# A four-layer graph network on one core: in each APPNP step, the sums of the last 9 node blocks by gathered rows beside products for the other 40

## The chip, the cores and the metric

The kernel runs on one core of a Trainium2 chip. A core has five engines with queues of their own: TensorE (PE, matmuls and transposes), VectorE (DVE), ScalarE (ACT), GpSimd (POOL; in this kernel it issues the gathers, that is DMAs whose addresses come from a list of row numbers) and SyncE (SP, which issues the other DMAs). The metric is device time in microseconds (us), lower is better, as the median of several runs. One more execution is taken by the profiler, and every row of a view below is from that one.

## The reference

A graph of 6250 nodes and 100000 edges (sorted by target `dst`), 128 features a node, passes through four layers, each of the form `x = x + layer(relu(layernorm(x)))`. The first is a mean over neighbours with a batch norm, the second a relational convolution (L1), the third an attention layer (L2). The change is in the fourth (L3), ten steps of APPNP:

```python
def _appnp(x, src, dst, norm, n_nodes):
    h = x
    def step(xk, _):
        msg = norm[:, None] * xk[src]
        agg = jax.ops.segment_sum(msg, dst, num_segments=n_nodes)
        return ((1.0 - ALPHA) * agg + ALPHA * h, None)
    xK, _ = jax.lax.scan(step, x, None, length=K)      # K = 10, ALPHA = 0.1
    return xK
...
src = jnp.concatenate([src, loop])                     # loop = arange(n): a self loop for each node
dst = jnp.concatenate([dst, loop])
...
norm = deg_inv_sqrt[src] * deg_inv_sqrt[dst]
return jax.nn.relu(_appnp(x, src, dst, norm, n))
```

So each step sums, for each node, the rows of its neighbours and its own, and mixes the first state in. The result of a step is what the next one reads.

## The kernel before

Nodes are padded to 49 blocks of 128 (`W`, 49). The kernel keeps z, the state times the root of the inverse degree, so that a step is z' = 0.9 / degree x (sum of z over edges and the self loop) + 0.1 x z of the start. The sum is a matrix product with the count matrix of edges. This matrix is made once, during the first layer, block of targets by block of targets (`stag`, L1006), and stored in DRAM as fp8 with the self loops added (`adj`, `looped`, L1018 to L1021). In the same stage the `chores` (L856) prepare lists of indices in pieces, between the blocks' products.

An L3 step (L1357 to L1403) runs over 13 groups of target blocks (`groups`, L1351: ten of 4, three of 3). For a group it goes over the 49 source blocks in 7 chunks of 7 (`GS`). A chunk is loaded from `adj` on SP (`am`, L1363; 448 KB for a group of four), turned from fp8 to fp32r into `ar` on ACT (L1370) or DVE (L1368) in turn, and multiplied: for each source block two matmuls, with the high and the low part of z (`xs`, L1374), so 98 matmuls for a group, all into one PSUM tile. `ar` has a pad of 128 behind each source block (`GD + 1`), and what is written of it are 7 pieces. Then ACT copies the sums (`y`, L1379), PE transposes them back (`yt`, L1382), DVE scales them and adds `hd` (0.1 x the first z, kept in SBUF as `by_node`; L1387), and `split2` (L1345) makes the new high and low parts with DVE, ACT and DVE. The parts are in two sets, `parts[0]` and `parts[1]`, read and written in turn. The last step applies relu, adds the kept x and stores the output (L1392 to L1402). The order on the engines is set by the framework's scheduler from the program's order and pools. POOL has no work in this stage.

Gathers are used in L1 and L2. `gather` (L686) reads 128 rows from a table in DRAM, one to a partition, for one column of a list of row numbers. In L1 (L1088 to L1099) the edges are cut into 128 equal runs, a lane for each partition. Step by step each lane gathers its next edge's row, scales it, and adds the sum so far if the edge has the target of the one before (`same`, L1097, `rows <- prev * same + rows`). The tiles of running sums are stored to a table (`scan1`); a node's sum is then the entry of its last edge, plus, where its edges begin in an earlier lane, what that lane ended with.

`general` (L83) computes all of it another way, for graphs whose tables overflow; flags (`over`, `redo`) decide between the two.

Of the kernel before, what the change touches and what calls it, by code (L numbers as in the profile page):

```python
# [10 lines left out]
F32 = mybir.dt.float32  # L11
I32 = mybir.dt.int32
BF16 = mybir.dt.bfloat16
F16 = mybir.dt.float16
AF = mybir.ActivationFunctionType
OP = mybir.AluOpType
AX = mybir.AxisListType
PSUM = bass.MemoryType.PSUM
DVE = mybir.EngineType.DVE

N = 6250
D = 128
E = 100000
P = 125
W = N // P
# [9 lines left out]
H = 8  # L35
# [6 lines left out]
K_STEPS = 10  # L42
ALPHA = 0.1
# [6 lines left out]
FW = 49  # L50
FN = FP * FW
# [11 lines left out]
LL = 782  # L63
LP = 128
# [8 lines left out]
F32R = mybir.dt.float32r  # L73
F8 = mybir.dt.float8e4
MULTI = 15
GD = 4
GS = 7
ENGINES = (mybir.EngineType.PE, mybir.EngineType.DVE, mybir.EngineType.Activation, mybir.EngineType.Pool,
# [553 lines left out]
def _fast(ctx, tc, a, out, pre):  # L632
    nc = tc.nc
    TT, TS, STT = nc.vector.tensor_tensor, nc.vector.tensor_scalar, nc.vector.scalar_tensor_tensor
    ident, eps, deg = pre["ident"], pre["eps"], pre["deg"]
    P, W = FP, FW
# [16 lines left out]
    def nodes(table):  # L653
        return table.rearrange("(w p) d -> p w d", p=P)
# [52 lines left out]

    table1 = dram.tile([FN * R, D], F32, name="ftable1")
# [4 lines left out]
    x_kept = dram.tile([FN, D], F32, name="x_kept")  # L713

    adj = dram.tile([W, P, W * P], F8, name="adj")
# [140 lines left out]
    def chores(sp):  # L856
# [6 lines left out]
        zero = sp.tile([LP, (LL + 2) * H // 4], F32, name="zero")  # L863
        nc.gpsimd.memset(zero, 0.0)
        for i in range(4):
            nc.sync.dma_start(begins.rearrange("(p q k) h -> q p (k h)", p=LP, q=4)[i], zero)
        nc.scalar.dma_start(scan1[ZROW:ZROW + 1, :], zero[0:1, :D])
        none = sp.tile([1, RW], F32, name="none")
# [42 lines left out]
        TS(end_row, row, float(ZROW), None, op0=OP.add)  # L911
        yield
# [8 lines left out]
    with tc.tile_pool(name="bxs", bufs=1) as bx, tc.tile_pool(name="bps", bufs=2, space=PSUM) as bps, \  # L921
# [64 lines left out]
        for w in range(W + 1):  # L986
# [29 lines left out]
            if w < W:  # L1016

                looped = bst.tile([P, P], F8, name="looped")  # L1018
                TT(looped, stag[:, w, :], eye, OP.add, saturate=False)
                nc.sync.dma_start(adj[w], stag.rearrange("p s d -> p (s d)"))  # L1020
                nc.sync.dma_start(adj[w][:, w * P:(w + 1) * P], looped)  # L1021
                behind = stag
# [221 lines left out]
    with tc.tile_pool(name="fl2f", bufs=2) as fp, tc.tile_pool(name="fl2fps", bufs=1, space=PSUM) as pp, \  # L1244
# [79 lines left out]
        def part5(b):  # L1324
            w0, n = blocks[b]
            t = fp.tile([P, 4, D], F32, name="z_hi")[:, :n, :]
            TS(t.bitcast(I32), z0[b].bitcast(I32), -4096, None, op0=OP.bitwise_and)
            nc.scalar.copy(parts[0][:, w0:w0 + n, 0, :], t)
            TT(parts[0][:, w0:w0 + n, 1, :], z0[b], t, OP.subtract)
            TS(by_node[:, w0:w0 + n, :], z0[b], ALPHA, None, op0=OP.mult)  # L1330
# [3 lines left out]
    mid.close()  # L1334


    hd = by_node
# [5 lines left out]
    parts.append(last.enter_context(tc.tile_pool(name="fl3x1", bufs=1)).tile([P, W, 2, D], F32R, name="xr1"))  # L1343

    def split2(pool, at, src):  # L1345
        t = pool.tile([P, D], F32, name="split_t")
        TS(t.bitcast(I32), src.bitcast(I32), -4096, None, op0=OP.bitwise_and)
        nc.scalar.copy(at[:, 0, :], t)
        TT(at[:, 1, :], src, t, OP.subtract)

    groups = [(w, 4) for w in range(0, 40, 4)] + [(w, 3) for w in range(40, W, 3)]  # L1351
    with tc.tile_pool(name="fl3a", bufs=3) as ap, tc.tile_pool(name="fl3c", bufs=3) as cp, \
            tc.tile_pool(name="fl3y", bufs=2) as yp, tc.tile_pool(name="fl3s", bufs=3) as sp, \
            tc.tile_pool(name="fl3ps", bufs=3, space=PSUM) as pp, \
            tc.tile_pool(name="fl3pt", bufs=2, space=PSUM) as pt, tc.tile_pool(name="fl3e", bufs=2) as ep:
        turn = 0
        for step in range(K_STEPS):  # L1357
            xs, new = parts[step % 2], parts[1 - step % 2]
            for w0, nd in groups:
                ps = pp.tile([D, GD * P], F32, name="dense3")  # L1360
                for s0 in range(0, W, GS):
                    am = ap.tile([P, GD, GS * P], F8, name="am")
                    nc.sync.dma_start(am[:, :nd, :],  # L1363
                                      adj[w0:w0 + nd, :, s0 * P:(s0 + GS) * P].rearrange("w p c -> p w c"))
                    ar = cp.tile([P, GS, GD + 1, P], F32R, name="ar")[:, :, :GD, :]
                    frm = am[:, :nd, :].rearrange("p w (s c) -> p s w c", c=P)
                    if turn % 2:
                        nc.vector.tensor_copy(ar[:, :, :nd, :], frm)  # L1368
                    else:
                        nc.scalar.copy(ar[:, :, :nd, :], frm)  # L1370
                    turn += 1
                    for i in range(GS):
                        for part in range(2):
                            nc.tensor.matmul(ps[:, :nd * P], xs[:, s0 + i, part, :],  # L1374
                                             ar[:, i, :nd, :].rearrange("p w c -> p (w c)"),
                                             start=(s0 + i == 0 and part == 0),
                                             stop=(s0 + i == W - 1 and part == 1))
                y = yp.tile([D, GD * P], F32, name="y3")
                nc.scalar.copy(y[:, :nd * P], ps[:, :nd * P])  # L1379
                yt = pt.tile([P, GD, D], F32, name="yt3")  # L1380
                for i in range(nd):
                    nc.tensor.transpose(yt[:, i, :], y[:, i * P:(i + 1) * P], ident)  # L1382
                if step < K_STEPS - 1:
                    for i in range(nd):
                        w = w0 + i
                        z = sp.tile([P, D], F32, name="z3")
                        STT(z, yt[:, i, :], d9[:, w:w + 1], hd[:, w, :], op0=OP.mult, op1=OP.add)  # L1387
                        split2(sp, new[:, w], z)
                    continue
                z = ep.tile([P, GD, D], F32, name="z3e")[:, :nd, :]  # L1390
                xb = ep.tile([P, GD, D], F32, name="x_back")[:, :nd, :]
                nc.sync.dma_start(xb, nodes(x_kept)[:, w0:w0 + nd, :])  # L1392
                for i in range(nd):
                    w = w0 + i
                    STT(z[:, i, :], yt[:, i, :], d9[:, w:w + 1], hd[:, w, :], op0=OP.mult, op1=OP.add)
                    nc.scalar.activation(z[:, i, :], z[:, i, :], AF.Relu, scale=back[:, w:w + 1])
                TT(xb, xb, z, OP.add)
                n = min(nd, full - w0)
                nc.sync.dma_start(nodes(out[0:full * P, :])[:, w0:w0 + n, :], xb[:, :n, :])
                if n < nd:  # L1400
                    nc.sync.dma_start(out[full * P:N, :], xb[:tail, n, :])
    last.close()  # L1402
    right.close()  # L1403
# [3 lines left out]
def gnn4_kernel(ctx: ExitStack, tc: tile.TileContext, a: dict, out: bass.AP):  # L1407
# [21 lines left out]
    with tc.tile_pool(name="csr", bufs=1) as sp, tc.tile_pool(name="csr2", bufs=4) as sp2, \  # L1429
# [87 lines left out]
        STT(over, most, float(HALO) + 0.5, over, op0=OP.is_gt, op1=OP.max)  # L1517
        bad_t = pp2.tile([1, EP], F32, name="p_ps")
# [67 lines left out]
```

## Time and profile before

| what | us |
| --- | --- |
| three runs | 6796.05, 6800.26, 6802.65 |
| their median | 6800.26 |
| the profiled execution | 6811.35 |
| its span, first to last instruction | 6809.6 |
| stage of L0 that builds `adj` (250 to 840) | 590 |
| the table of L1 (840 to 1220) | 380 |
| gathers of L1 (1220 to 2350) | 1130 |
| gathers of L2 (2510 to 3815) | 1305 |
| rest of L2 and the start of L3 (3815 to 4004.57) | 189.57 |
| the ten steps of L3, first to last matmul (4004.57 to 6799.20) | 2794.63 |

The stages were cut by hand from the timeline, and the busy time of each engine was then asked for each stage. Rows of groups of instructions have the line, the engine, the operation, out <- in with the program's names, shapes and count; behind the bar the busy time in all (us), the mean of one (ns), and the idle time of that engine just before such instructions with what ended it. A row of the timeline or of the chain of waits begins with its start and its length in us. PEclk is the share of the full clock that PE was granted: 1.00 in L3, 0.50 in the gather stages, 0.792 over the span.

### The profile page before, as it was taken

The numbers are of one execution on the slowest core, as the hardware profiler recorded it, in microseconds if no ns is written. First come the engines' busy times: TensorE is split into PE (matmuls) and PEld (weight loads), VectorE is DVE, ScalarE is ACT, GpSimd is POOL, SyncE is SP. The second block draws the span as 40 slices with busy tenths as digits, with TensorE's granted clock in tenths as the row PEclk, the third lists the DMA queues.
The fourth block names the chain that finished last, engine by engine and source line by source line (L and its number), as shares of the span: only waits on it lengthen the run. The fifth ranks groups of instructions, "written<-read, shape, count | busy, mean of one in ns | idle before, by whom it ended". The sixth has DMA issues, their size and how long they took to land.

```text
span 6809.6 us, 58963 instructions
## 1 busy us (share of the span) xinstructions
PE 3979.7 (58%) x19527; PEld 3092.1 (45%) x19527; DVE 3147.4 (46%) x7607; ACT 2727.3 (40%) x4424; POOL 1930.8 (28%) x1823
## 2 busy tenths in 40 slices
PE   3899899100000020000000379999999999999999
PEld 3466644000000010000000158888888888888888
DVE  7976543222222234545454654444444444444443
ACT  0667643222222220000000465555555555555555
POOL 1000000677777766776767400000000000000000
PEclk8799999555555555555555699999999999999999
DMA  2111166322222222322222234555545555455555
GB/s 62 65 69 68 64 268 289 133 99 93 93 96 90 89 63 79 100 89 91 95 93 89 76 95 138 145 140 143 141 138 144 143 141 143 138 145 141 141 154 146
DMA packets 590194, 805.02 MB, mean 118 GB/s; under 512 B 59275, under 2 KB 532626, under 8 KB 570422
## 3 DMA queue, kind: packets, MB, share of 16 engines
q1 hardware_dynamic: 521968, 677.37, 31.2%
q0 software_dynamic: 57728, 119.10, 6.4%
q10 hardware_dynamic: 10182, 4.69, 0.3%
q8 instruction: 155, 2.54, 0.2%
q14 instruction: 161, 1.32, 0.1%
HBM read 529.94 MB, written 274.22 MB: 118 GB/s over the span
## 4 chain that ended last, share of the span: by engine, by line
PE 54%; POOL 16%; DVE 11%; issue 9%; another core or an unknown queue 3%; ACT 2%; DMA 1%; POOLq 1%; DVEq 0%; SPq 0%; ACTq 0%
PE dense L1374 40%; POOL rows L687 15%; PE hr_ps L1074 5%; PE dense L955 5%; DVE rows L1231 3%; DVE rows L1215 2%; PE cnt_ps L1002 1%; PE yt L1382 1%; POOLq L687 1%; DVE rows L1209 1%; DVE far L1207 1%; ACT stag L1006 1%; DMA rows<-ftable,lane_src 0%; DVE fwr L916 0%
## 5 line engine op out<-in xcount | busy, mean ns | idle before, releaser
L1374 PE MATMUL dense<-ar,xr 128*128 128x512 f32 (+1 forms) x12740 | 2768.5, 378 | 20.7 <-ACT ar L1370 20.7
L1374 PEld LDWEIGHTS dense<-ar,xr 128*128 128x128 f32 x12740 | 2342.2, 188 | 398.4 <-ACT ar L1370 20.9
L1370 ACT CAST ar<-am 128x3584 fp32r<-128x3584 fp8e4 (+1 forms) x455 | 1373.1, 3018 | 834.1 <-PE dense L1374 633.8
L1368 DVE CAST ar<-am 128x3584 fp32r<-128x3584 fp8e4 (+1 forms) x455 | 987.2, 2170 | 1367.2 <-ACT ar L1370 1000.7
L687 POOL DMA_INDIRECT rows<-ftable,rel_l x822 | 876.6, 1066 | 1285.3 <-DMA w<-in_L_gnn_W_dram 1035.1
L687 POOL DMA_INDIRECT rows<-ftable,lane_src x822 | 883.8, 1075 | 403.4 <-issue 256.6
L1289 PE MATMUL ht_ps<-ident_p,h1g 128*128 128x128 f32 x49 | 9.8, 295 | 1333.5 <-ACT h1g L677 1333.2
L695 PE MATMUL ht_ps<-ident_p,long 128*128 128x128 f32 x49 | 16.5, 446 | 1193.1 <-issue 1183.6
L1094 ACT ACTIVATE rows<-rows,lane_norm 128x128 f32<-128x128 f32 x822 | 327.2, 401 | 811.3 <-DMA rows<-ftable,rel_l 651.6
L1097 DVE SCALAR_TENSOR_TENSOR rows<-rows,same 128x128 f32<-128x128 f32 x770 | 270.9, 352 | 805.6 <-issue 450.7
L1289 PEld LDWEIGHTS ht_ps<-ident_p,h1g 128*128 128x128 f32 x49 | 6.6, 144 | 1342.4 <-issue 1337.2
L695 PEld LDWEIGHTS ht_ps<-ident_p,long 128*128 128x128 f32 x49 | 9.9, 206 | 1199.4 <-issue 1187.0
L955 PE MATMUL dense<-xs,stag 128*128 128x384 bf16 x2401 | 448.5, 327 | 34.3 <-ACT stag L1006 34.1
L1006 ACT ACTIVATE stag<-cnt_ps 128x392 fp8e4<-128x392 f32 x784 | 381.7, 494 | 171.7 <-PE cnt_ps L1002 170.9
L1231 DVE SCALAR_TENSOR_TENSOR rows<-rows,same 128x136 f32<-128x136 f32 x770 | 271.9, 353 | 184.5 <-remote 60.1
L1074 PE MATMUL hr_ps<-fwr,ht 128*128 128x512 f32 x784 | 342.3, 597 | 6.2 <-ACT ht L697 6.2
L955 PEld LDWEIGHTS <-stag 128*128 128x128 fp8e4 x2401 | 227.3, 97 | 165.1 <-ACT stag L1006 45.2
L982 DVE TENSOR_TENSOR hot_v<-key_v,iota_v 128x1568 bf16<-128x1568 bf16 x196 | 190.8, 974 | 120.3 <-PE cnt_ps L1002 120.3
L1186 ACT COPY cut<-cut 128x136 f32<-128x136 f32 (+1 forms) x52 | 15.7, 305 | 570.3 <-DVE up L1199 273.0
L1074 PEld LDWEIGHTS hr_ps<-fwr,ht 128*128 128x128 f32 x784 | 148.8, 191 | 192.5 <-issue 180.3
L1077 DVE COPY hr<-hr_ps 128x512 f32<-128x512 f32 x196 | 135.6, 692 | 204.1 <-PE hr_ps L1074 201.6
L1215 DVE TENSOR_TENSOR rows<-rows 128x128 f32<-128x128 f32 x822 | 189.0, 284 | 47.4 <-issue 45.0
(268 smaller groups left out, 3292.3 us busy)
## 6 DMA issues: line engine op xcount, KB each, us to landing
am<-adj SPq DMA_DIRECT2D x700, 448.0 KB
ftable<-hr SPq DMA_DIRECT2D x49, 2048.0 KB
am<-adj SPq DMA_DIRECT2D x210, 336.0 KB
scan<-rows SPq DMA_DIRECT2D x51, 1152.0 KB
scan<-rows SPq DMA_DIRECT2D x51, 1024.0 KB
adj<-stag SPq DMA_DIRECT2D x49, 784.0 KB
rows<-ftable,rel_l POOLq DMA_INDIRECT x822
rows<-ftable,lane_src POOLq DMA_INDIRECT x822
```

What stands on the lines that cost most here:

```text
L687: nc.gpsimd.indirect_dma_start(out=tile_, out_offset=None, in_=table, in_offset=bass.IndirectOffsetOnAxis(ap=idx[:, k:k + 1], axis=0))
L955: nc.tensor.matmul(ps, stag[:, s, :], xs[:, s].rearrange("p t d -> p (t d)"), start=(s == 0), stop=(s == W - 1))
L982: TT(hot, k[:, :, None, :].to_broadcast(shape), iota[:, None, :, :].to_broadcast(shape), OP.is_equal)
L1006: nc.scalar.activation(stag[:, :, at:at + 2 * GN].rearrange("p s (g d) -> p g s d", g=2), ps[:, i, :2 * HG].rearrange("p (g s d) -> p g s ...
L1074: nc.tensor.matmul(ps, ht1[b][:, i * P:(i + 1) * P], wr[:, 4 * q:4 * q + 4, :], start=True, stop=True)
L1094: nc.scalar.activation(rows[:, t, :], rows[:, t, :], AF.Copy, scale=norm_l[:, k:k + 1])
L1097: STT(rows[:, t, :], prev, same[:, k:k + 1], rows[:, t, :], op0=OP.mult, op1=OP.add)
L1215: TT(rows[:, t, :D].rearrange("p (h c) -> p h c", h=H), rows[:, t, :D].rearrange("p (h c) -> p h c", h=H), rows[:, t, D:SW, None].to_broad ...
L1231: STT(rows[:, t, :SW], rows[:, t - 1, :SW], same[:, k0 + t:k0 + t + 1], rows[:, t, :SW], op0=OP.mult, op1=OP.add)
L1368: nc.vector.tensor_copy(ar[:, :, :nd, :], frm)
L1370: nc.scalar.copy(ar[:, :, :nd, :], frm)
L1374: nc.tensor.matmul(ps[:, :nd * P], xs[:, s0 + i, part, :], ar[:, i, :nd, :].rearrange("p w c -> p (w c)"), start=(s0 + i == 0 and part == ...
```

## The change

Products are made for the first 40 blocks of targets only (`DW`), in 10 groups of four: 70 chunks a step rather than 91. `adj` has 40 blocks. The sums of the last 9 blocks (`TW`) are made as in L1: the edges from number 81,440 (`E0`) on are cut into 128 lanes of 145 (`LE`), and a step gathers their rows from z in DRAM (`collect`, 29 tiles of 5 columns), runs the sum along each lane on DVE (`run_on`, 144 operations), stores the tiles to `scan3` and the lanes' ends to `carry3` (`put_down`), gathers the sums of the nodes' last edges and the carried sums (`fetch_ends`, 18 gathers), and adds the node's own row for the self loop (`add_up`). So z must also lie in DRAM, and every step stores it (`z_at`, two tables in turn); 0.1 x the first z is there too (`z_first`) and is fetched for each group, rather than kept in SBUF.

Other parts: `am` is loaded two chunks at a time (14 source blocks, 896 KB; the chunk 4 of a group alone), 40 loads a step. `ar` has no pad, so a chunk is written as one run of 3584 elements. Every third cast is on DVE, the others are on ACT. The first two groups do their chunks 0 to 4 before either does 5 and 6, which read the gathered blocks' parts of the step before. Splits work on a whole group (128x512) rather than a block. And the order on every engine is written out: each piece of work is put into `plan` with an expected time in chunks of products, the list is sorted by it, and the instructions are issued in this order with the scheduler off. In the `chores` come the lists of the new lanes, and a guard sends graphs with more than `128 x 145` edges in the last 9 blocks to `general`.

```diff
+GL = 14
+DW = 40
+TW = FW - DW
+LE = 145
+E0 = E - LP * LE
+LC = 5
...
+    z_at = [dram.tile([FN, D], F32, name=f"z_at{i}") for i in range(2)]
+    z_first = dram.tile([FN, D], F32, name="z_first")
+    scan3 = dram.tile([LP * LE + 1, D], F32, name="scan3")
+    carry3 = dram.tile([LP + 1, D], F32, name="carry3")
+
+    adj = dram.tile([DW, P, W * P], F8, name="adj")
...
+        dst_e = sp.tile([LP, LE], I32, name="dst_e")
+        nc.sync.dma_start(dst_e, a["dst"][E0:].rearrange("(p k) -> p k", k=LE))
+        nc.sync.dma_start(src_e, a["src"][E0:].rearrange("(p k) -> p k", k=LE))
...
+        nc.vector.memset(same_e[:, 0:1], 0.0)
+        TT(same_e[:, 1:], dst_e[:, 1:], dst_e[:, :LE - 1], OP.is_equal)
...
-            TS(by_node[:, w0:w0 + n, :], z0[b], ALPHA, None, op0=OP.mult)
+            nc.sync.dma_start(nodes(z_at[0])[:, w0:w0 + n, :], z0[b])
+            t = fp.tile([P, 4, D], F32, name="z_al")[:, :n, :]
+            TS(t, z0[b], ALPHA, None, op0=OP.mult)
+            nc.sync.dma_start(nodes(z_first)[:, w0:w0 + n, :], t)
...
-                    ar = cp.tile([P, GS, GD + 1, P], F32R, name="ar")[:, :, :GD, :]
-                    frm = am[:, :nd, :].rearrange("p w (s c) -> p s w c", c=P)
-                    if turn % 2:
...
+    def rows_behind(time, step, w0, n, at):
...
+        def fetch():
+            at["first"] = pool.tile([P, wide, D], F32, name=f"first3{kind}")
+            nc.sync.dma_start(at["first"], nodes(z_first)[:, w0:w0 + n, :])
+
+        def scale():
+            z = at["z"] = at["more"] if kind else pool.tile([P, wide, D], F32, name="z3")
+            for i in range(n):
+                STT(z[:, i, :], at["sums"][:, i, :], d9[:, w0 + i:w0 + i + 1], at["first"][:, i, :],
+                    op0=OP.mult, op1=OP.add)
...
+            TS(t.bitcast(I32), z.bitcast(I32), -4096, None, op0=OP.bitwise_and)
+            TT(new[:, :, 1, :], z, t, OP.subtract)
...
+                nc.scalar.copy(new[:, :, 0, :], at["t"])
...
+                nc.sync.dma_start(nodes(z_to)[:, w0:w0 + n, :], at["z"])
...
+        then(time - 3, fetch)
+        then(time, scale)
+        then(time + 0.6, keep)
+        then(time + (1.2 if out_at else 0.5), store)
+
+
+    order = [(g, c) for c0, c1 in ((0, 5), (5, 7)) for g in (0, 1) for c in range(c0, c1)]
+    order += [(g, c) for g in range(2, DW // GD) for c in range(7)]
...
+        wide = GS if c == 4 else 2 * GS
+        am = ap.tile([P, GD, 2 * GS * P], F8, name="am")
...
+        ar = casts[key] = cp.tile([P, GS, GD, P], F32R, name="ar")
+        frm = loads.pop(key).rearrange("p w (s c) -> p s w c", c=P)
+        if n % 3 == 2:
+            nc.vector.tensor_copy(ar, frm)
+        else:
+            nc.scalar.copy(ar, frm)
...
+    def collect(step, k, tiles):
+
+        tiles[k] = rp.tile([LP, LC, D], F32, name="rows3")
+        for t in range(LC):
+            gather(tiles[k][:, t, :], z_at[step % 2], src_e, k * LC + t)
+
+    def run_on(k, tiles):
+
+        for t in range(LC):
+            col = k * LC + t
+            if col:
+                prev = tiles[k][:, t - 1, :] if t else tiles[k - 1][:, LC - 1, :]
+                STT(tiles[k][:, t, :], prev, same_e[:, col:col + 1], tiles[k][:, t, :], op0=OP.mult, op1=OP.add)
+
+    def put_down(k, tiles):
+        nc.sync.dma_start(scan3[0:LP * LE].rearrange("(p k) d -> p k d", k=LE)[:, k * LC:(k + 1) * LC, :], tiles[k])
+        if (k + 1) * LC == LE:
+            nc.sync.dma_start(carry3[1:LP + 1, :], tiles[k][:, LC - 1, :])
+
+    def fetch_ends(w0, at):
+
+        at["got"], at["more"] = (ep.tile([P, 3, D], F32, name=f"{k}3") for k in ("got", "more"))
+        for i in range(3):
+            gather(at["got"][:, i, :], scan3, end_e, w0 - DW + i)
+            gather(at["more"][:, i, :], carry3, carry_e, w0 - DW + i)
+
+    def fetch_own(step, w0, at):
+        at["own"] = ep.tile([P, 3, D], F32, name="own3")
+        nc.sync.dma_start(at["own"], nodes(z_at[step % 2])[:, w0:w0 + 3, :])
+
+    def add_up(at):
+        TT(at["got"], at["got"], at["more"], OP.add)
+        TT(at["got"], at["got"], at["own"], OP.add)
+        at["sums"] = at["got"]
+
+    for step in range(K_STEPS):
+        for at, (g, c) in enumerate(order):
+            n, key = step * NP + at, (step, g, c)
+            if c in (0, 2, 4, 5):
+                then(n - 4.8, load, key)
+            then(n - 2, cast, key, n)
+            then(n, product, key, 0, 3)
+            then(n + 0.45, product, key, 3, GS)
+            if c == 6:
+                state = {}
+                then(n + 1, evict, g, state)
+                then(n + 1.4, turn_back, state)
+                rows_behind(n + 1.75, step, g * GD, GD, state)
+        tiles, n = {}, step * NP
+        for k in range(LE // LC):
+            there = n + 1.91 * k + 6.5
+            then(max(there - 8, n + 1.3), collect, step, k, tiles)
+            then(there, run_on, k, tiles)
+            then(there + 0.8, put_down, k, tiles)
+        for j in range(TW // 3):
+            state, w0, there = {}, DW + 3 * j, n + 65.2 + 2.3 * j
+            then(there - 3.2, fetch_ends, w0, state)
+            then(there - 2.5, fetch_own, step, w0, state)
+            then(there, add_up, state)
+            rows_behind(there + 0.05, step, w0, 3, state)
+    with tc.manual_schedule():
+        for _, _, do, args in sorted(plan, key=lambda p: p[:2]):
+            do(*args)
...
+        least = sp.tile([FW, 1], F32, name="p_least")
+        nc.gpsimd.memset(least, float(E0) - 0.5)
+        nc.gpsimd.affine_select(least, least, pattern=[[0, 1]], compare_op=OP.is_ge, fill=-1.0,
+                                base=-DW, channel_multiplier=1)
+        TT(least, base, least, OP.is_lt)
+        TT(over, over, least, OP.max)
```

The unit of the times is one chunk of products, 14 matmuls.

## What the change should do to the time

> **What bounds the kernel now.** I read the sums of busy time first, then the busy time by stage, then the chain of waits inside one L3 step, then the groups of instructions that the change touches. No engine is busy over the whole span, so the stages have different limits. The rows of the view by stage give start:end, length, and the busy time of PE, PEld, DVE, ACT and POOL, then the granted clock, the DMA share and GB/s:
>
> ```profile
> PE 3979.7 (58%) x19527; PEld 3092.1 (45%) x19527; DVE 3147.4 (46%) x7607; ACT 2727.3 (40%) x4424; POOL 1930.8 (28%) x1823
> ...
> 840.00:1220.00 380.00, 357.57 (x883) 163.10 (x883) 162.45 (x343) 164.45 (x296) 0.00 (x0) 0.97 0.65 272
> 1220.00:2350.00 1130.00, 0.00 (x0) 0.00 (x0) 286.38 (x814) 327.24 (x822) 876.55 (x822) 0.50 0.29 95
> ...
> 4004.57:6799.20 2794.63, 2794.62 (x13227) 2389.85 (x13227) 1287.15 (x1836) 1543.07 (x1070) 0.00 (x0) 1.00 0.51 143
> ```
>
> The last row is the ten L3 steps. PE has no idle time in them at clock 1.00, POOL does nothing, DVE and ACT work half of the time. The chain of waits (start, us, what) says the same; the first three pieces are groups of four blocks, the last two groups of three:
>
> ```profile
> 4724.77 22.24 PE dense L1374 x98
> 4747.01 0.44 PE yt L1382 x4
> 4747.45 22.24 PE dense L1374 x98
> ...
> 4792.80 17.02 PE dense L1374 x98
> 4810.23 17.01 PE dense L1374 x98
> ```
>
> A step is 10 x (22.24 + 0.44) + 3 x (17.02 + 0.42) = 279.2 us; ten by the stage row are 2794.6, so 279.5 each. All else of the span is 6809.6 - 2794.6 = 4015.0.
>
> **What the change removes.** The last 9 blocks' products (3 x 17.44) leave PE, which keeps 10 x 22.68 = 226.8 us a step. That is the lowest a step can be.
>
> **What it puts on POOL.** 145 gathers of rows and 18 of segment ends in each step. A gather's price is in the timeline of the two stages that gather now (start, us, engine, operation, idle before it):
>
> ```profile
> 1500.81 1.10 POOL L687 DMA_INDIRECT rows<-ftable,rel_l  x1 [0.30 <-issue]
> 1502.21 1.09 POOL L687 DMA_INDIRECT rows<-ftable,rel_l  x1 [0.30 <-issue]
> ...
> 2706.54 0.94 POOL L687 DMA_INDIRECT rows<-ftable,lane_src  x1 [0.30 <-issue]
> 2707.79 0.94 POOL L687 DMA_INDIRECT rows<-ftable,lane_src  x1 [0.30 <-issue]
> ```
>
> Undisturbed, one takes 0.94 + 0.30 = 1.25 us. In the L1 stage, where each gather has one DVE row sum beside it (L1097), the slot is 1.40, 0.15 more. Two other places show what DVE does to a gather:
>
> ```profile
> 2511.21 6.68 DVE L1237 TENSOR_TENSOR long<-long,row_in_L_gnn_b_gat_dram 128x6272 f32<-128x6272 f32 x1
> 2512.28 6.45 POOL L687 DMA_INDIRECT rows<-ftable,lane_src  x1 [0.30 <-issue]
> ...
> 3912.89 0.41 DVE L1330 TENSOR_SCALAR long<-z 128x512 f32<-128x512 f32 x1
> 3913.02 1.09 POOL L687 DMA_INDIRECT got<-scan,end_row  x1 [0.30 <-issue]
> ```
>
> A gather that starts under a DVE operation with two SBUF sources, or under a scalar one that does 512 elements in 0.41 us (two per cycle), ends 0.8 us after that operation. So 163 x 1.25 = 203.8 us a step; port waits at the 144 row sums between 0 and 144 x 0.15 = 22, of which I take 9, because the order puts the five sums of a tile in one burst of 5 x 0.35 = 1.8 us, over which one gather or two start; other two-source operations (splits, adds) some 3. Idle on POOL, twice a step: the end gathers wait for the last tile (landing 1.6 us as at 2347.4 to 2349.0, one sum 0.35, a store's landing 3.3, from 161.7 us over 49 waits at L1021) = 5.3, and the next step's first gather waits for the last 9-block store (1.6 + adds and scaling 1.1 + split 0.9 + 3.3) = 6.9. POOL's sum: 203.8 + 9 + 3 + 12.2 = 228 us, a bare 1 over PE.
>
> **DVE and ACT.** The rows of the two casts, and two DVE operations that differ in shape alone:
>
> ```profile
> L1370 ACT CAST ar<-am 128x3584 fp32r<-128x3584 fp8e4 x350 | 1116.7, 3191 | 658.0 <-PE dense L1374 508.1 <-issue 137.8 <-ACT xr L1348 7.0
> L1368 DVE CAST ar<-am 128x3584 fp32r<-128x3584 fp8e4 x350 | 802.5, 2293 | 1099.8 <-ACT ar L1370 800.5 <-PE dense L1374 289.4 <-DMA am<-adj 6.5
> ...
> L880 DVE TENSOR_SCALAR cut<-same 128x816 f32<-128x816 f32 x1 | 1.0, 973 | 0.0
> L792 DVE TENSOR_SCALAR p_ok<-p_loc 128x1664 f32<-128x1664 f32 x1 | 1.0, 1010 | 0.0
> ```
>
> There are 70 casts a step, 46.7 on ACT and 23.3 on DVE (it has every third). ACT: 46.7 x 3.19 + evictions and copies some 13 = 162 us, two casts (6.4 us) in every three units of PE's work (9.7 us), so it has room. On DVE a cast is 2.29 us now, faster than an element per cycle: a two-per-cycle form. L880, whose source is one run and whose target is in pieces, does 816 elements in the time in which L792 does 1664. After, the pad in `ar` is gone: the target of the cast is one run of 3584, its source still pieces, so it is L880's case reversed. Bounds: 2.29 (as now) and 3.84 (one per cycle: 0.15 + 3584 x 1.03 ns, the slope from 128x128 and 128x512 TENSOR_TENSORs, 0.286 and 0.684 us). I take 3.84, and no hold on gathers, since an operation with one SBUF source at 3853.43 left the gather at 3853.82 its 0.94. DVE's sum is 23.3 x 3.84 + 144 x 0.352 + scaling, splits and adds 33 = 174 us.
>
> One rule speaks against the change. The Trainium skill, page "SBUF — State Buffer", section "Who interferes with whom", says that DVE in a mode with two ports keeps the shared pair for the whole instruction and GpSimd is blocked fully, DMA descriptors included; by it a cast at 2.29 us would cost POOL most of its length. The trace agrees where a gather starts under such an operation (3912.89, 3913.02), but the scalar one at 3912.54 left the gather begun at 3911.78 at 0.94. The page "VectorE: DVE Perf Modes", section "What auto-detection actually checks", gives the mode to outermost dims both even or equal: here 7 against one run, so by it the cast is slow and harmless.
>
> **Where the engines wait for each other.** Each queue now has one order. On DVE a cast stands behind the sums of a tile, and these wait for gathers; while POOL is later than the plan (1.91 units of 226.8/70 = 3.24 us for 5 gathers, so 1.24 a gather), DVE's casts and so PE run at POOL's pace. On top, DVE has a cast every 9.7 us against three units, two ahead of the product: of the 6.48 us of lead 3.84 are the cast, 2.6 are left, and a tile's sums (1.95) plus a group's scaling (2.3) in front take 4.25, 1.6 too much. That may happen for each of 10 groups: 0 to 16 us; I take 7, as not every group meets a tile. On SP a store behind a tile's sums holds later loads, but these go 4.8 units (15 us) ahead. On PE the return transposes stand 0.4 unit after the eviction (0.6 us for 1.3). ACT's copies wait for a split of 0.4 us with casts behind them, in the same lead.
>
> DMA: per step 40 loads move the 32.1 MB that 70 of 91 loads moved, with packets twice as long; with 163 gathers of 64 KB and as much stored, and 13 fetches and stores of z, some 60 MB in 235 us is 255 GB/s. The L1 table stage moved 272 at a share of 0.65, so it fits; what is lost if not lies in the wider case below.
>
> **Sum.** 228 + 7 = 235 us a step. Outside: the first load is double, +2 us (PE's start waits for it; 4.44 us now at 4001.34); more index work and a guard on DVE, +1, as the rest lies beside PE in the build stage (DVE 415 of 590 us); the alpha products are stored rather than kept, on SP, which is idle there. So span = 4018 + 10 S. The profiled execution took 6811.35 with a span of 6809.6, the median of the runs is 6800.26, 9.3 below the span: time = 4008.7 + 10 S. With S = 235 that is 6359, say **6360**.
>
> **The rivals.**
> PE alone bounds (0.15): bursts of sums meet no gather start and no cast is late, S = 226.8, time 6277. For it: POOL's sum is equal within its bounds. Against: a POOL later than its plan by 1% already shows.
> Gathers at the L1 slot throughout (0.23): 163 x 1.40 + 3 + 12.2 + 7 = 250, time 6510. For it: all of the L1 stage is so (1130 us for 822 is 1.375), and DMA is busier here. Against: L1 spreads its sums, here they are in bursts.
> The cast stays at two per cycle and holds POOL (0.09): a gather that would start under it loses 2.29 - 0.62 (half a slot) = 1.67, 23.3 times = 39, S = 228 + 39 = 267, time 6679. For it: even or equal dims could be judged otherwise than I read L880.
> Slower (0.09): both of these on POOL, 163 x 1.40 + 39 + 3 + 12.2 = 282.4, time 6833. It decides from a mean slot of (279.2 - 12.2 - 3)/163 = 1.62 us. Against: DVE at 2.29 a cast would have more room, and L1's slot comes without bursts.
> That the change does not do what it says (0.01): a step keeps 279 us, or the fallback for a full table runs; nothing in the rows speaks for it.
>
> **How the numbers follow.** Forecast 0.43, and 0.15 + 0.23 + 0.09 + 0.09 + 0.01. The range from 6275 to 6540 holds the forecast (S 230 to 241), PE alone and the L1 slot with 3 us a step more for DMA, 0.81 together. A measurement of this kernel tells from no change what is over 0.2%, 13.6 us. Faster: 0.43 + 0.15 + 0.23 + 0.09 = 0.90; same 0.02 (the last rival and the edge of the slower one); slower 0.08.
>
> **What would show it.** PE's matmuls in a step add up to 226.8; L3's stage row shows POOL at 150 to 200 busy per step and PE idle by 8 us a step, put down to casts of DVE. The DVE cast's mean: 3.8 or 2.3. The mean gather beside L3's casts: 0.94 to 1.0, and 1.1 in the L1 case. POOL's two idle times per step near 5 and 7 us; if the first gather of a step waits for a dense group's store instead, PE bounds. I am wrong if gathers average over 1.3 us busy, if loads come late (casts waiting for `am`), or if the clock in L3 falls below 1.00.

## The result and the profile after

The changed kernel takes 7214.52 us (median of four runs, 7198.23 to 7258.53), the kernel before 6798.16 beside it: 1.062 times as long, with a 95% interval of 1.058 to 1.067. The forecast was 6360, faster.

The first lines of the page of the kernel after, its span and the busy time of each engine:

```profile
span 7213.1 us, 56507 instructions
...
PE 3701.3 (51%) x16497; PEld 2695.1 (37%) x16497; DVE 3556.8 (49%) x8248; ACT 2777.8 (39%) x4082; POOL 3482.4 (48%) x3456
```

PE does 278 us less than before in a span that is 404 us longer. The view by stage of the same kernel (start:end, length, busy time of PE, PEld, DVE, ACT, POOL, granted clock, DMA share, GB/s) puts all of it into L3:

```profile
840.00:1220.00 380.00, 357.37 (x882) 163.03 (x882) 160.97 (x340) 164.22 (x296) 0.97 (x1) 0.97 0.65 273
1220.00:2350.00 1130.00, 0.00 (x0) 0.00 (x0) 286.97 (x815) 325.48 (x822) 875.04 (x821) 0.50 0.29 95
2510.00:3815.00 1305.00, 0.00 (x0) 0.00 (x0) 608.80 (x2584) 42.86 (x153) 891.57 (x835) 0.50 0.29 93
3998.80:7201.90 3203.10, 2523.64 (x10196) 1998.06 (x10196) 1690.72 (x2463) 1595.83 (x724) 1542.36 (x1624) 0.88 0.60 186
```

The ten steps last 3203.1 us, 320.3 each, where they took 279.5; outside them are 4010.0 us, where 4015.0 were and 4018 had been forecast. No engine is busy throughout the steps: PE for 252.4 of 320.3 us, POOL for 154, DVE for 169, ACT for 160. PE's idle time is 67.9 us a step, and its clock, 1.00 before, is 0.88 on the average, so that the products themselves take 25.6 us more than the 226.8 they need at full clock. 226.8 + 25.6 + 67.9 is the step.

The costliest groups of L3 in the kernel after (line, engine, operation, count, then busy time in us and the mean of one in ns, then the idle time before them and what ended it):

```profile
L1489 PE MATMUL dense<-ar,xr 128*128 128x512 f32 x9800 | 2486.5, 413 | 495.0 <-issue 217.4 <-ACT ar L1480 205.4 <-DVE ar L1478 69.6
...
L693 POOL DMA_INDIRECT rows<-z_at,src_e x1450 | 1376.8, 950 | 1374.4 <-DVE rows L1513 659.6 <-issue 479.9 <-DMA scan<-rows 92.3
...
L1478 DVE CAST ar<-am 128x3584 fp32r<-128x3584 fp8e4 x233 | 905.2, 3885 | 1128.8 <-remote 662.1 <-PE dense L1489 401.7 <-issue 54.9
...
L1513 DVE SCALAR_TENSOR_TENSOR rows<-rows,same_e 128x128 f32<-128x128 f32 x1160 | 409.7, 353 | 41.0
```

Each instruction costs what the forecast said: a gather 0.950 us, a cast on DVE 3.885, a row sum 0.353. The waits are new. PE waits for casts (ACT and DVE), casts for PE and for "remote" (a releaser that the profile can't name), POOL for row sums, and 217 us of PE's idle time have the releaser "issue": PE had nothing to wait for that the profile shows. A ring in which each waits for the next names no culprit. One stretch of the timeline of this kernel does (start us, length us, engine, line and operation, idle time before it):

```profile
5295.63 4.92 PE L1489 MATMUL dense<-ar,xr 128*128 128x512 f32 x20
...
5299.93 0.94 POOL L693 DMA_INDIRECT rows<-z_at,src_e  x1 [0.30 <-issue]
5301.18 0.95 POOL L693 DMA_INDIRECT rows<-z_at,src_e  x1 [0.30 <-issue]
5302.43 0.94 POOL L693 DMA_INDIRECT rows<-z_at,src_e  x1 [0.30 <-issue]
5303.68 0.95 POOL L693 DMA_INDIRECT rows<-z_at,src_e  x1 [0.30 <-issue]
5304.93 0.94 POOL L693 DMA_INDIRECT rows<-z_at,src_e  x1 [0.30 <-issue]
5305.85 3.18 ACT L1480 CAST ar<-am 128x3584 fp32r<-128x3584 fp8e4 x1 [14.93 <-remote]
...
5309.08 1.22 PE L1489 MATMUL dense<-ar,xr 128*128 128x512 f32 x2 [8.52 <-issue]
```

Between 5300.6 and 5305.9 nothing but POOL works. The cast at 5305.85 needs a tile that PE had read for the last time at 5293.98 by the trace, and its data had landed at 5286. It starts 12 us after the later of the two, by which time PE has run out of chunks. PE then starts again at half clock (a matmul every 0.43 us rather than 0.23).

### The profile page after: what moved, and what is told of

It reads as the page before. It is cut to its first block, busy times and chain, and to the rows that moved or that the text cites. A ratio compares the mean times of both kernels' runs of the same rounds, so it can differ in the third digit from the quotient of the medians.

```text
span 7213.1 us, 56507 instructions
## 1 busy us (share of the span) xinstructions
PE 3701.3 (51%) x16497; PEld 2695.1 (37%) x16497; DVE 3556.8 (49%) x8248; ACT 2777.8 (39%) x4082; POOL 3482.4 (48%) x3456
## 3 DMA queue, kind: packets, MB, share of 16 engines
q14 instruction: 189, 1.55, 0.1%
## 5 line engine op out<-in xcount | busy, mean ns | idle before, releaser
L1489 PE MATMUL dense<-ar,xr 128*128 128x512 f32 x9800 | 2486.5, 413 | 495.0 <-issue 217.4
L1489 PEld LDWEIGHTS dense<-ar,xr 128*128 128x128 f32 x9800 | 1943.7, 200 | 995.9 <-issue 291.9
L693 POOL DMA_INDIRECT rows<-z_at,src_e x1450 | 1376.8, 950 | 1374.4 <-DVE rows L1513 659.6
L1480 ACT CAST ar<-am 128x3584 fp32r<-128x3584 fp8e4 x467 | 1483.3, 3187 | 1357.8 <-remote 566.1
L1478 DVE CAST ar<-am 128x3584 fp32r<-128x3584 fp8e4 x233 | 905.2, 3885 | 1128.8 <-remote 662.1
L1513 DVE SCALAR_TENSOR_TENSOR rows<-rows,same_e 128x128 f32<-128x128 f32 x1160 | 409.7, 353 | 41.0
L1425 DVE SCALAR_TENSOR_TENSOR z<-yt,d,first 128x128 f32<-128x128 f32 x400 | 112.4, 345 | 266.9 <-PE yt L1499 218.0
```

The costliest lines, as they stand in the source:

```text
L693: nc.gpsimd.indirect_dma_start(out=tile_, out_offset=None, in_=table, in_offset=bass.IndirectOffsetOnAxis(ap=idx[:, k:k + 1], axis=0))
L1478: nc.vector.tensor_copy(ar, frm)
L1480: nc.scalar.copy(ar, frm)
L1489: nc.tensor.matmul(sums[g], parts[step % 2][:, s, part, :], casts[key][:, i].rearrange("p w c -> p (w c)"), start=(s == 0 and part == 0), ...
L1513: STT(tiles[k][:, t, :], prev, same_e[:, col:col + 1], tiles[k][:, t, :], op0=OP.mult, op1=OP.add)
```

## The experiments

Three theories stood after this. A: while POOL issues gathers one after the other, the other engines hear of each other late, or get few instructions through. B: signals are as ever, and the order written into `plan` couples the queues, since casts stand behind row sums and these behind gathers. C: a busy POOL as such, or the DMA traffic, slows the rest. Each time below is that of a single run, unless it says more, and stands beside the kernel before on the same chip.

**Without the row gathers.**

```diff
...
     def collect(step, k, tiles):
-        tiles[k] = rp.tile([LP, LC, D], F32, name="rows3")
-        for t in range(LC):
-            gather(tiles[k][:, t, :], z_at[step % 2], src_e, k * LC + t)
+        tiles[k] = held[k % 5]
```

> Leaves out the 145 row gathers of a step (the row sums run over five tiles of zeros, so the last 9 blocks' sums are wrong); the row sums, their stores, the 18 gathers of ends and the order stay. Theory A, late signals (while POOL issues gathers one after the other, PE's completion signals come up to 20 us late, and casts, evictions and then PE wait for them): the products run without gaps for most of the step, S near 235, 6300 to 6450 us. Theory B, fixed order (signals are as ever; DVE's casts wait behind row sums which wait for gathers): the sums wait for nothing either, S near 230, 6250 to 6400 us. Both fall if it stays above 6900: then stores, loads or the order alone cost it.

Measured: 6322.43 us beside 6792.18. The ten steps in the view by stage of this run:

```profile
3975.10:6305.20 2330.10, 2290.21 (x10196) 1883.55 (x10196) 1682.88 (x2459) 1601.26 (x724) 172.04 (x180) 0.99 0.69 215
```

A step is 233.0 us, with PE busy for 229.0 at a clock of 0.99. DVE and ACT do the same work as in the kernel after, and the order is the same. So the loads, the stores, the row sums and the order cost 6 us a step together, and the 145 gathers 87.

**POOL busy with memsets, without row gathers.**

```diff
-            gather(tiles[k][:, t, :], z_at[step % 2], src_e, k * LC + t)
+            nc.gpsimd.memset(tiles[k], 0.0)
```

> POOL is as busy as with gathers but issues no DMA for the rows: each of the 145 gathers of a step is replaced by a memset of a row tile (128x640) on POOL, so the last 9 blocks' sums are wrong. Theory A in the narrow form (it is the DMA issue by POOL that makes signals late): no late signals, S set by PE or by 145 memsets, whichever is longer, 6300 to 6600 us. Theory C (a busy POOL of any kind, by its port or its writes, holds the others): as slow as the changed kernel, 7000 us or more. Theory B: as A.

Measured: 6333.82 us beside 6792.18. The memsets in the view of groups of this run:

```profile
L1505 POOL MEMSET rows<- 128x640 f32 x1450 | 926.3, 641 | 967.8 <-DVE rows L1513 550.5 <-DMA scan<-rows 277.7 <-ACT z L683 72.7
```

They took 0.64 us each, so POOL was busy for 93 us a step, where the gathers had kept it busy for 138. The time is 11 us over that of the run without gathers: theory C falls for a POOL that works this much and merely writes into SBUF.

**Without the row sums on DVE.**

```diff
-            then(there, run_on, k, tiles)
```

> Leaves out the 144 row sums of a step on DVE (so the last 9 blocks' sums are wrong); gathers, stores and order stay, and no cast stands behind a sum that waits for a gather. Theory B: the coupling is gone, S near 230 to 240, 6300 to 6400 us. Theory A: POOL's gathers run with fewer pauses, PE's signals are as late or later, 6900 us or more.

Measured: 7196.55 us beside 6792.18. No cast stands behind a sum now, and the time is that of the kernel after to 0.3%. Two groups of this run:

```profile
L1489 PE MATMUL dense<-ar,xr 128*128 128x512 f32 x9800 | 2487.8, 412 | 601.5 <-issue 314.3 <-ACT ar L1480 194.6 <-DVE ar L1478 90.5
...
L693 POOL DMA_INDIRECT rows<-z_at,src_e x1450 | 1375.0, 948 | 1409.5 <-DMA scan<-rows 739.4 <-issue 533.9 <-DMA z_first<-z_al 76.2
```

POOL's wait for row sums (660 us) has become a wait for stores (739 us), and PE's idle time is 67.9 us a step as before (3193.4 us for the ten steps, 2514.5 busy). The sum that POOL waited for was a symptom, and the casts' place behind the sums is no cause. SP's order, in which stores stand ahead of later loads, still couples the queues here; the next run has no such coupling at all.

**Gathers that nobody waits for, in the kernel before.** POOL gets some 145 gathers a step into tiles that are never read; everything else is the kernel before, in which PE had no gap.

```diff
...
                     turn += 1
+                    for i in range(2 if turn % 5 else 0):
+                        gather(gp.tile([LP, D], F32, name="idle_rows"), scan1, end_row, (2 * turn + i) % W)
```

> The kernel before with some 145 gathers a step added on POOL (random rows of a table, 128x512 bytes each, into tiles that nobody reads), nothing else changed and no row sum; they run in the first 1.8 ms of the ten steps, as nothing holds them back. Theory A: PE, which was never idle in these steps, gets gaps while the gathers run; 1.8 ms slowed by 10 to 40%, 7000 to 7500 us. Theory B: nobody waits for these gathers, 6800 to 6830 us. A cost by DMA traffic alone would lie between.

Measured: 8228.41 us beside 6792.18, 1436 us for 1456 gathers, more than theory A had expected; theory B, by which nothing should have been lost, falls as the cause. The stretches of this run by the view by stage:

```profile
4000.00:4450.00 450.00, 450.00 (x2092) 379.58 (x2091) 209.70 (x303) 249.06 (x170) 361.92 (x290) 1.00 0.67 184
4600.00:5800.00 1200.00, 193.27 (x421) 113.77 (x419) 42.34 (x57) 47.65 (x32) 925.95 (x871) 0.51 0.21 59
6130.00:8215.00 2085.00, 2084.99 (x9903) 1786.37 (x9902) 957.99 (x1355) 1152.33 (x802) 0.00 (x0) 1.00 0.53 143
```

There are two regimes. In the first 450 us PE runs as if nothing were there, with 290 gathers beside it of 1.25 us on the average (361.92 / 290): DVE's casts hold many of them. From 4600 to 5800 POOL issues 871 gathers, one in 1.38 us, and PE gets through 421 matmuls in the time in which it had done 5600. DMA traffic is no cause: in the bad stretch it is 59 GB/s. The timeline of this run in the bad stretch, and after the last gather:

```profile
4713.20 1.96 POOL L687 DMA_INDIRECT idle_rows<-scan,end_row  x1 [0.30 <-issue]
...
4713.68 1.76 DVE L1369 CAST ar<-am 128x2688 fp32r<-128x2688 fp8e4 x1 [76.64 <-remote]
...
4714.71 7.20 PE L1377 MATMUL dense<-ar,xr 128*128 128x384 f32 x27
...
4721.70 0.94 POOL L687 DMA_INDIRECT idle_rows<-scan,end_row  x1 [0.30 <-issue]
4722.01 0.19 PEld L1377 LDWEIGHTS dense<-ar,xr 128*128 128x128 f32 x1 [0.42 <-issue]
4722.95 0.94 POOL L687 DMA_INDIRECT idle_rows<-scan,end_row  x1 [0.30 <-issue]
4723.41 0.34 PE L1377 MATMUL dense<-ar,xr 128*128 128x384 f32 x1 [1.50 <-issue]
4724.20 0.94 POOL L687 DMA_INDIRECT idle_rows<-scan,end_row  x1 [0.30 <-issue]
4724.81 0.19 PEld L1377 LDWEIGHTS dense<-ar,xr 128*128 128x128 f32 x1 [2.61 <-issue]
...
4726.21 0.33 PE L1377 MATMUL dense<-ar,xr 128*128 128x384 f32 x1 [2.46 <-issue]
...
6041.10 1.10 POOL L687 DMA_INDIRECT idle_rows<-scan,end_row  x1 [0.30 <-issue]
...
6048.51 0.59 PE L1377 MATMUL dense<-ar,xr 128*128 128x512 f32 x1 [2.90 <-issue]
...
6070.42 4.76 PE L1377 MATMUL dense<-ar,xr 128*128 128x512 f32 x11
```

A weight load at 4722.01, its matmul at 4723.41, the next weight load at 4724.81, its matmul at 4726.21: one PE instruction in 1.40 us, in the middle of a chunk, where none waits for data. Just before, after the gather at 4713.20 had been held for 1.0 us (1.96 rather than 0.94), PE did some 30 weight loads and 30 matmuls without a gap, first one in 0.32 us, then one in 0.17. So it isn't only late signals: the engine's own next instruction doesn't come. Nor does it end with the last gather, which is over at 6042.2: PE goes on in single instructions to 6048.51, and works without a break only from about 6070 on. Theory A in this sharper form, starved engines, was put to the next runs.

**Pauses between idle gathers.** The same kernel with four small memsets on POOL after every four gathers (0.29 us each).

```diff
...
+                    if turn % 5 in (1, 3):
+                        for _ in range(4):
+                            nc.gpsimd.memset(pause, 0.0)
```

> The kernel before with the same idle gathers, and after every four of them four small memsets on POOL (128x128). Theory A: most of the 1436 us that the gathers cost is gone, 6800 to 7100 us. If the cost is that of the gathers' number or their data: still over 8000 us.

Measured: 6799.93 us beside 6793.67. Of 1436 us, 6 are left, with as many gathers and as many bytes. PE's matmuls and the pauses in the view of groups of this run:

```profile
L1381 PE MATMUL dense<-ar,xr 128*128 128x512 f32 x9800 | 2255.1, 391 | 20.9 <-ACT ar L1372 20.9
...
L1376 POOL MEMSET pause<- 128x128 f32 x1456 | 425.0, 292 | 72.9 <-ACT z L677 72.1
```

**Plain DMAs from POOL.** As many DMAs of the same size from POOL's queue, of rows that lie side by side.

```diff
-                        gather(gp.tile([LP, D], F32, name="idle_rows"), scan1, end_row, (2 * turn + i) % W)
+                        rows = gp.tile([LP, D], F32, name="idle_rows")
+                        nc.gpsimd.dma_start(rows, scan1[(2 * turn + i) % W * P:((2 * turn + i) % W + 1) * P, :])
```

> The kernel before with as many idle DMAs of the same size issued by POOL, but of rows that lie side by side (no list of row numbers). If any DMA issued by POOL starves the others: near 8200 us. If it is the indirect form alone: 6790 to 6850 us.

Measured: 6793.19 us beside 6793.67; the group of these DMAs:

```profile
L1375 POOL DMA_DIRECT2D idle_rows<-scan x1456 | 955.1, 664 | 156.8 <-ACT z L677 72.4 <-DMA idle_rows<-scan 52.8 <-issue 29.2
```

They followed one another in 0.71 us on the average, closer than the gathers, and nothing was lost. So it is the gather that starves the others, not any DMA from POOL; its list of row numbers and its scattered rows were not separated.

**Pauses in the changed kernel.** Two memsets of a row tile ahead of the five gathers that fill it.

```diff
         tiles[k] = rp.tile([LP, LC, D], F32, name="rows3")
+        nc.gpsimd.memset(tiles[k], 0.0)
+        nc.gpsimd.memset(tiles[k], 0.0)
         for t in range(LC):
```

> The changed kernel with two memsets on POOL (128x640, 0.64 us each in the run with memsets for gathers) ahead of every five gathers, nothing left out. Theory A, now sharper: while gathers follow each other without a pause, the other engines get about one instruction for a gather (in the run with idle gathers PE issued one in 1.40 us), and a pause of a microsecond lets them fill up again. Then POOL needs 163 x 1.25 + 29 x 1.9 + 15 = 274 us at most, PE no longer starves, S 245 to 280, 6450 to 6800 us. If instead the sheer number of gathers takes the time from PE, the pauses only add, 7200 to 7700 us.

Measured: 6684.74 us beside 6793.67; more work on POOL, and 530 us less than the kernel after. The ten steps of this run, and the gathers and memsets in the view of groups:

```profile
3985.30:6666.80 2681.50, 2407.07 (x10196) 1948.65 (x10196) 1684.24 (x2459) 1602.70 (x725) 1927.78 (x2201) 0.94 0.72 222
```

```profile
L693 POOL DMA_INDIRECT rows<-z_at,src_e x1450 | 1387.1, 957 | 563.4 <-issue 364.0 <-DMA z_at<-z 119.3 <-POOL rows L1505 76.1
...
L1504 POOL MEMSET rows<- 128x640 f32 x290 | 190.3, 656 | 78.3 <-ACT z L683 77.8 <-issue 0.3
...
L693 POOL DMA_INDIRECT got<-scan,end_e x90 | 86.6, 963 | 117.9 <-DMA carry<-rows 86.5 <-issue 26.8 <-DVE more L1425 4.6
```

POOL's wait for row sums is gone, PE's idle time is down from 67.9 to 27.4 us a step (2681.5 - 2407.1), and the row gathers of a step take 221 us from first to last, pauses included, where they took 255 without.

**Fewer and other pauses.** One memset for five gathers, one for ten, and one for five with the row sums a unit later in the order.

```diff
+        if k % 2 == 0:
+            nc.gpsimd.memset(tiles[k], 0.0)
```

> As the run with two memsets ahead of every five gathers, with one of them (0.64 us). Theory A: the pause need only be long enough for the other engines to fill up. If 0.64 us is enough, the 145 row gathers of a step take about 209 us rather than 220, a step 258 rather than 268, some 6590 us. If it is too short, PE starves in part: over 6685 us.

> One memset for every ten gathers. In the run with idle gathers PE issued some 60 instructions at full speed after a pause (7 us of products) and then one in 1.40 us. Theory A with such a store of instructions: ten gathers last 12.5 us, so PE starves for some 5 of 13 us, S 270 to 310, 6700 to 7100 us, slower than one memset for five. If the store is larger than that: as fast as or faster than one for five.

```diff
-            then(there, run_on, k, tiles)
-            then(there + 0.8, put_down, k, tiles)
+            then(there + 1.0, run_on, k, tiles)
+            then(there + 1.5, put_down, k, tiles)
```

> As with one memset, and the row sums stand one unit later in the order, their stores 0.7 unit (with two memsets PE waited 21 us a step for casts on DVE, and DVE's sums waited 48 us a step for gathers, with casts behind them). Theory B as a second-order term: up to 10 us a step less than with one memset at the old places, 6490 to 6590 us. If the row tiles come free too late for POOL instead: slower than it.

Measured, beside 6788.18 (the first and the last row repeat runs from above, beside 6798.16 and 6793.67):

| memsets of 0.64 us | us | row gathers of a step, first to last |
| --- | --- | --- |
| none (the kernel after) | 7214.52 | 255 us |
| one for ten gathers | 7037.33 | 244 |
| one for five | 6893.16 | 231 |
| one for five, sums a unit later | 6966.14 | 236 |
| two for five | 6684.74 | 221 |

The less POOL pauses, the longer its own gathers take, since what they wait for is starved. One memset for five is too short: 6590 us had been expected if it was enough, and it came over 6685, the other branch. Later row sums were expected to bring 6490 to 6590 and made it worse by 73 us, as the row tiles come free later (POOL's wait for row sums ahead of its memsets rose from 258 to 348 us).

**A cast that holds the gathers.** 16 elements of padding, so that DVE's cast writes seven pieces again.

```diff
-        ar = casts[key] = cp.tile([P, GS, GD, P], F32R, name="ar")
+        ar = cp.tile([P, GS, GD * P + 16], F32R, name="ar")[:, :, :GD * P]
+        ar = casts[key] = ar.rearrange("p s (w c) -> p s w c", c=P)
```

> The changed kernel with 16 elements of padding behind each source block of the fp32r tile, so that the cast on DVE writes seven pieces again (2.29 us before, 3.89 after). In the run with idle gathers, PE ran at full speed as long as such casts held the gathers up (mean gather 1.27 us), and starved when they stopped. Theory A: each of the 23 casts of a step holds POOL for about 1.7 us and so feeds the others: S 250 to 300, 6500 to 7000 us, clearly under the changed kernel. If a hold by DVE is no such pause, or only adds to POOL's time: 7200 us or more.

Measured: 6858.51 us beside 6793.67, 356 us less than the kernel after. The cast and the gather in the view of groups of this run:

```profile
L1479 DVE CAST ar<-am 128x3584 fp32r<-128x3584 fp8e4 x233 | 539.7, 2316 | 1045.3 <-PE dense L1490 442.7 <-remote 412.3 <-issue 180.6
...
L693 POOL DMA_INDIRECT rows<-z_at,src_e x1450 | 1546.5, 1067 | 928.5 <-issue 459.3 <-DVE rows L1514 267.4 <-DMA z_first<-z_al 75.0
```

The cast is back at 2.316 us, the gathers are held (1.067 us rather than 0.950), and the kernel is faster. A hold of a gather can let the others fill up as a pause does, as at 4713 above. But the cast itself is also 1.57 us shorter, 23 times a step, and this run doesn't separate the two. The Trainium skill, page "VectorE: DVE Perf Modes", section "What auto-detection actually checks", asks for outermost dims both even or equal before two elements are done per cycle; 16 elements, which make them 7 and 7, decide here between 3.885 and 2.316 us, as it says.

**The version with two memsets, timed.**

> The kernel with two memsets ahead of every five gathers once more, timed in rounds against the kernel before, since one look showed 6685 beside 6794 us. Theory A (POOL's chain sets the step: 220 us of gathers and pauses and some 49 us of ends, stores and first landing): 6670 to 6700 us, 1.3 to 1.8% under the kernel before. If the one look was chance: within 0.5% of it.

Measured: 6686.97 us (median of four runs, 6681.12 to 6692.73) beside 6800.1, a ratio of 0.9835, interval 0.9818 to 0.9851. It is under both kernels, under the one before by 1.65%.

## Why the prediction was wrong

*What the change removes*: right. PE was busy for 229.0 us a step once the gathers were out, for a forecast of 226.8. *Outside the steps*: 4010.0 for 4018.

*The cast*: right; 3.885 us for 3.84, and it holds no gather (mean 0.950). *A gather's price on POOL*: right, 0.95 + 0.30. *The coupling of the queues*: 7 were put down, and with the gathers out a step is 233.0 us, 6 over PE. That run has no sum that waits for a gather, so it shows only the part that comes from the order itself.

*The step that failed* is the one under "What it puts on POOL". It counted a gather as 1.25 us of POOL's time, with a wait at DVE's port as its only tie to other engines, and made the step the longer of POOL's sum (228) and PE's (226.8). A run of gathers without a pause keeps PE, DVE and ACT from going on: with 1456 gathers that nobody waits for, the kernel before lost 1436 us, and with pauses between them 6. In the changed kernel this comes back to POOL, which waits 66 us a step for row sums that DVE can't do (659.6 us in the group row), and to PE as 67.9 us of idle time and 25.6 of low clock. That 233.0 without gathers is near the forecast's 235 is luck: POOL's sum of 228 has no part in it. Of its signs of being wrong the clock came (0.88, under 1.00), while the gathers stayed at 0.950.

A smaller term of the same sum was short as well. POOL's two idle times in a step were put at 5.3 and 6.9 us; in the run with two memsets, where POOL no longer waits for row sums, they are 8.7 and 11.9 (`carry<-rows` 86.5 and `z_at<-z` 119.3 over ten steps). So some 8 us a step are missing from it even where the others are not starved.

A sign stood in the trace of the kernel before, in the L1 stage that was taken as the price list. The group of its row sums:

```profile
L1097 DVE SCALAR_TENSOR_TENSOR rows<-rows,same 128x128 f32<-128x128 f32 x770 | 270.9, 352 | 805.6 <-issue 450.7 <-ACT rows L1094 254.7 <-remote 85.1
```

and its timeline:

```profile
1771.43 1.09 POOL L687 DMA_INDIRECT rows<-ftable,rel_l  x1 [0.30 <-issue]
...
1772.56 0.35 DVE L1097 SCALAR_TENSOR_TENSOR rows<-rows,same 128x128 f32<-128x128 f32 x1 [1.06 <-issue]
...
1772.83 1.12 POOL L687 DMA_INDIRECT rows<-ftable,rel_l  x1 [0.30 <-issue]
1773.96 0.35 DVE L1097 SCALAR_TENSOR_TENSOR rows<-rows,same 128x128 f32<-128x128 f32 x1 [1.05 <-issue]
```

DVE is idle for 450.7 us with nothing to wait for that the profile shows ("issue"), and a sum starts when a gather ends: 1772.56 after 1771.43 + 1.09, 1773.96 after 1772.83 + 1.12. Three quarters of the 821 sums start within 60 ns of a gather's end, and in the median 9.25 us after ACT had their row ready. The prediction read the slot of 1.40 us as 1.25 plus a port wait at the sum. That reading falls. The run with idle gathers has no row sum, and by its trace 480 of its 870 slots from 4600 to 5800 are 1.40 us long; in 235 of these no instruction of PE, DVE or ACT begins. Three in a row:

```profile
5214.40 1.09 POOL L687 DMA_INDIRECT idle_rows<-scan,end_row  x1 [0.30 <-issue]
5215.80 1.09 POOL L687 DMA_INDIRECT idle_rows<-scan,end_row  x1 [0.30 <-issue]
5217.20 1.09 POOL L687 DMA_INDIRECT idle_rows<-scan,end_row  x1 [0.30 <-issue]
```

What makes a slot 1.40 us stays open. That DVE's idle time in L1 is the same starving is likely, not shown: no run changed that stage. POOL sets the pace there, so it costs nothing, and the row looked like a price.

*The rivals.* "Gathers at the L1 slot" did not come: the gathers stayed at 0.95 us. "Slower" (6833) had the direction, by a cause that did not come: casts at two per cycle that hold POOL. They took 3.885 us and held none, and in the run with padding, where they do hold POOL, the kernel is 356 us faster. DMA was no limit: the bytes were right (186 GB/s over 320.3 us are 59.6 MB a step, for 60), and 222 GB/s were moved in the run with two memsets.

*The skill.* Its page "SBUF — State Buffer", section "Who interferes with whom", was weighed as speaking against the change, by DVE locking out GpSimd. The cost ran the other way, from POOL's gathers to all the others, and no run here puts it down to that port: 1450 memsets by POOL, which write SBUF, cost 11 us in all.

## What stays open

What the engines share with an indirect gather isn't shown. The runs show that it is not POOL being busy with memsets, nor a POOL DMA as such (plain DMAs), nor the traffic, and that gathers go well as long as something holds them up now and then (the first 450 us of the run with idle gathers). A slow fetch of instructions is not seen either: in the bad stretch the three 16 KB packets of an instruction queue took 0.95 to 1.17 us, and 0.96 is their median over that run. Whether a pause as such matters, or only that gathers come more seldom, was not separated: they came one in 1.55 us in the good 450 us and one in 1.65 with pauses, but one in 1.38 in the bad stretch. Why PE went on in single instructions after the last gather is open too. Whether late signals (5305.85 in the kernel after) and missing instructions (4722 to 4726 in the run with idle gathers) are one thing was not separated. Why the run with idle gathers went well for its first 450 us and then tipped is only argued: once PE is behind, DVE has no casts, and nothing holds the gathers any more.

## What to carry to other kernels

A row of a stage is a price only for the engine that sets that stage's pace; what the others pay has to be looked for in their idle time, and idle time put down to "issue" beside a busy POOL is a warning. Before gathers are laid beside dense work, put idle ones into the kernel that stands and see what it loses: one run, and here it showed a loss of 1436 us. If gathers must run beside other engines, try giving POOL some 1.2 us of something else for every four or five of them; in these two kernels that was enough to get under, or back to, the kernel before.

## What the runs showed of the hardware

- Gathers with a row list on POOL, one in 1.25 to 1.40 us without a pause, kept the other engines from going on: in 1200 us of such gathers PE did 421 matmuls rather than some 5600, for long stretches one instruction in 1.40 us.
- After a gather that was held for 1.0 us PE issued some 60 instructions without a gap.
- Pauses of 1.2 us after four gathers took the loss from 1436 us to 6; with 0.64 us ahead of five the changed kernel is 105 us slower than the one before, with 1.28 us it is 113 us faster.
- Plain DMAs from POOL (0.664 us each) cost the others nothing that shows (6793.19 beside 6793.67 us); memsets on POOL (0.64 us) in place of the gathers cost 11 us.
- After its pause of 8.5 us at 5309 PE issued matmuls in 0.43 us rather than 0.23; the mean granted clock of the steps fell from 1.00 to 0.88.
